# Issuing the second layer's weight loads from SyncE, spread over the first edge slots, in a two-layer graph transformer kernel

## The chip, the cores and the metric

The kernel runs as one program on one core of a Trainium2 chip. The core has five engines that work side by side, each on its own in-order queue of instructions: TensorE (PE, matrix products; its weight loads are listed apart as PEld), VectorE (DVE), ScalarE (ACT), GpSimd (POOL) and SyncE (SP, which issues transfers). Transfers run on 16 DMA engines that all queues share. The metric is the time of one execution on the device in microseconds (us). The kernel before took 2957.67 us, the median of 3 runs (2949.06 to 2958.34).

## The reference

The reference is a graph network with 6250 nodes, 128 features, 100000 edges (sorted by their destination), 16 node types and 32 edge types. Two layers are applied, and then an output product and a normalization:

```
k, q, v = typed_linear(x, ntype, Wk / Wq / Wv)        # one 128x128 matrix per node type
kT = einsum('nhd,htdo->nhto', k, Watt)                # for every node, 8 heads, 32 edge types
vT = einsum('nhd,htdo->nhto', v, Wmsg)
a  = sum(kT[src, :, etype] * q[dst]) * pri[:, etype].T / sqrt(16)
att = softmax of a over the edges of each destination
hag = segment_sum(vT[src, :, etype] * att, dst)
h = silu(typed_linear(hag, ntype, Wa)); h = h * alpha + x * (1 - alpha)
h = layernorm(h) * g + b
# after both layers: out = layernorm(x + (h @ ff_w + ff_b))
```

All data are float32. Each of the two layers has its own Wk, Wq, Wv, Wa, Watt, Wmsg and pri.

## The kernel before

**Tables.** For every node and each of the 32 edge types the kernel stores one row of 256 numbers in HBM: the key already multiplied by Watt and pri, and the value by Wmsg. An edge then needs one row, picked by its source and its type. The table of layer 1 (`tabs[0]`) is made at the start, while the edges are ranked. The table of layer 2 (`tabs[1]`) is made during layer 1: as soon as a block of nodes has its new features, their keys and values and table rows are computed (`nodes`, then `pieces_of` and `table_block`) and stored by GpSimd (line 1915). In the code layer 1 is `l == 0`.

**Weights in SBUF.** There is one set of tiles for both layers. `wkqv[:, 0]` and `wkqv[:, 1]` hold Wk and Wv, `bdk` and `bdv` hold Watt and Wmsg as blocks on a diagonal (the rest is zero, so each is cleared by a memset before it is loaded), and `prit` holds pri. So the second layer's weights can only be loaded when the first layer's table is complete, and they must be there when the first block of layer 1 makes its table rows. `scale_edge_weights` (lines 253 and 254) multiplies `bdk` by `prit` once they are loaded; for the second layer it is written in `nodes`, after the first block's normalization.

**Edges.** Nodes are sorted by type class and by degree into blocks of 128, and a *visit* handles up to four such blocks (a superblock). A *slot* is one edge of each of 128 nodes: GpSimd gathers 128 table rows into one of 50 places of a ring, `kv` (line 1691). VectorE multiplies several slots by the query of the block (line 1707), sums over the 16 numbers of each head (line 1712), takes the softmax with ScalarE's help, multiplies the values by it and adds them up (lines 1518, 1529, 1534). A place of the ring is free again when its values are added. The query of a block is copied to PSUM by ScalarE (line 1471), from a query that TensorE made for the superblock (line 292, copied by ScalarE at lines 1167 and 1171).

**Order.** GpSimd's instructions run in the order in which they are written. The other engines' instructions are put into order by an automatic planner: what is written earlier goes first among what it holds ready, and a later instruction can be pulled up into a gap. Within the visits other work is interleaved with the slots: `spread` enters a generator with a number of steps and a number of slots, and `tick`, called once for each slot, advances the first generator of each list by its share. `work` holds the next queries and the node steps, `pieces` the table rows of layer 2, and `extra` the look-up `looked`. The look-up finds, for the first superblocks of layer 2, which edges come from nodes that will be ready early. It writes two small arrays to HBM (line 1282) and reads them back in many broadcast loads on SyncE (line 1302) that VectorE compares (lines 1326 and 1333). It is spread over 62 slots.

**The loads that the change touches.** After the first table is complete, `tile_gnn_kernel` calls `arm(True)`, which issues Wk and Wv by `load_typed` (line 236) and eight heads' Watt, Wmsg and pri by `load_edge_weights` (lines 245, 246, 248), and then enters `edges()`. These are 2 + 3 x 8 = 26 transfers, for the second layer all on ScalarE's queue. Since they are written ahead of the edges, they are ahead of ScalarE's first copy of a query.

Of the kernel before, what the change touches and what calls it, by code (L numbers as in the profile page):

```python
# [54 lines left out]
HALF = 64  # L55

LOOK = 62.0

OWN_TAILS = {0: ((23, 76, 1, 52),)}

# [33 lines left out]
def kernel(  # L94
# [21 lines left out]
    nc = tc.nc  # L116
# [6 lines left out]
    _, H, RT, HS, _ = Watt.shape  # L123
# [100 lines left out]
    wkqv, wq0, wa = weights[:, :3], weights[:, 3], weights[:, 4]  # L224

    bdk = wts.tile([P, RT, 2 * HS], F32, name="bdk")
    bdv = wts.tile([P, RT, 2 * HS], F32, name="bdv")
    prit = wts.tile([P, RT], F32, name="prit")
# [6 lines left out]
    def load_typed(to, w):  # L235
        nc.scalar.dma_start(to, w.rearrange("t d o -> d t o"))

    def load_edge_weights(l, heads=range(H)):
        if heads[0] == 0:
            nc.vector.memset(bdk, 0.0)  # L240
            nc.vector.memset(bdv, 0.0)
        for h in heads:
            s = slice(h * HS, (h + 1) * HS)
            c = slice((h % 2) * HS, (h % 2 + 1) * HS)
            nc.scalar.dma_start(bdk[s, :, c], Watt[l, h].rearrange("t d o -> d t o"))
            (nc.scalar if l else nc.sync).dma_start(bdv[s, :, c],
                                                    Wmsg[l, h].rearrange("t d o -> d t o"))
            (nc.scalar if l else nc.sync).dma_start(prit[s, :],
                                                    pri[l, h:h + 1, :].to_broadcast([HS, RT]))

    def scale_edge_weights():

        nc.vector.tensor_scalar(prit, prit, 1.0 / float(HS) ** 0.5, None, op0=ALU.mult)
        nc.vector.tensor_tensor(bdk, bdk, prit.unsqueeze(2).to_broadcast([P, RT, 2 * HS]),
                                op=ALU.mult)
# [146 lines left out]
    with tc.manual_schedule(engines={mybir.EngineType.Pool, mybir.EngineType.DVE,  # L402
# [5 lines left out]
        nc.gpsimd.iota(nodef, pattern=[[P, NT]], base=0, channel_multiplier=1,  # L408
                       allow_small_or_imprecise_dtypes=True)
        load_edge_weights(0, range(3))  # L410
        nc.vector.tensor_copy(colf, coli)
        nc.vector.tensor_copy(rowf, rowi)
# [74 lines left out]
        for sl in cuts:  # L487
# [4 lines left out]
            for i in range(sl.start, sl.stop):  # L492
                nc.tensor.matmul(inv_ps, row1[:, i], col1[:, i, :2],
                                 start=(i == 0), stop=(i == NT - 1))
        load_edge_weights(0, range(3, H))
        load_later()
        zeros = pp.tile([P, 2 * D], F32, name="zeros")
# [215 lines left out]
    with tc.manual_schedule(engines={mybir.EngineType.Pool}):  # L713
# [380 lines left out]
        got, stage = [], ""  # L1094
# [22 lines left out]
    def arm(fast):  # L1117
# [56 lines left out]
        def queries0(got, i0, k, types):  # L1174
            ntb, hr = types_of(i0, k), old_rows(xrd, i0, k, "hq")
            yield HOP
            hT = transposed(nps, lambda i: hr[:, i, :], k)
            yield HOP
            ps = nps.tile([P, SB * P], F32, name="nb")
            yield from typed_steps(npl, types, ntb, hT, k * P, [(ps, wq0)])  # L1180
            yield HOP
            q = yield from q_rows(ps, k, "q")
            got.append((q, ntb))
# [44 lines left out]
        def edges():  # L1228
# [160 lines left out]
                nc.vector.tensor_scalar(again, one_bad, 0.0, None, op0=ALU.is_gt)  # L1389
                yield  # L1390

            got, work, pieces, extra = {}, [], [], []
            for _ in queries0(got.setdefault(0, []), *visits[0][1]):
                pass

            def spread(of, gen, steps, slots):

                of.append([gen, steps / slots, 0.0, 1.0])

            def tick(n):  # L1400
                for of in (work, pieces, extra):
                    if of:
                        w = of[0]
                        w[2] += w[1] * n
                        while w[2] >= w[3]:
                            w[2] -= w[3]
                            weight = next(w[0], of)
                            if weight is of:
                                of.pop(0)
                                break  # L1410
                            w[3] = weight or 1.0

            done = []
            spread(extra, looked(), 27, LOOK)

            def rush(of, gen):
                while any(w[0] is gen for w in of):
                    for _ in of.pop(0)[0]:
                        pass
# [185 lines left out]
            for v, (l, (i0, k, types), part, e) in enumerate(visits):  # L1605
# [29 lines left out]
                for i in range(k):  # L1635
# [67 lines left out]
                    for bundle in bundles:  # L1703
                        for (j0, j1, lanes), kv in zip(bundle, [bring(*c[:2]) for c in bundle]):
                            c = j1 - j0
                            kk = kv[:lanes, :, :D]
                            nc.vector.tensor_tensor(  # L1707
                                kk, kk, q[:lanes].unsqueeze(1).to_broadcast([lanes, c, D]),
                                op=ALU.mult)
                            for r in range(c):  # L1710
                                if r == c // 3:
                                    nc.vector.tensor_reduce(  # L1712
                                        a[:lanes, j0:j1, :],
                                        kk.rearrange("p k (h d) -> p k h d", h=H),
                                        axis=AX.X, op=ALU.add)
                                step()
                                tick(1.0)
                            leave(c / CH)
# [311 lines left out]
        if not fast:  # L2030
            for i, w in enumerate((Wk, Wv)):
                load_typed(wkqv[:, i], w[0])
            load_typed(wq0, Wq[0])
            load_typed(wa, Wa[0])
            load_edge_weights(0)
            scale_edge_weights()
            for i0, k in superblocks(NT):
                n = k * P
                hr = old_rows(x, i0, k, "hr")
                nti4 = npl.tile([P, SB * P], I32, name="nti4")  # L2040
                nc.sync.dma_start(
                    nti4[:, :n], ntype[i0 * P:i0 * P + n].unsqueeze(0).to_broadcast([P, n]))
                hT = transposed(nps, lambda i: hr[:, i, :], k)
                outs = [nps.tile([P, SB * P], F32, name="nb") for _ in range(2)]
                typed_linear(npl, range(TY), nti4, hT, n, [(outs[j], wkqv[:, j]) for j in range(2)])
                for j in range(2):
                    to = npl.tile([P, SB * P], F32, name=f"kvT{j}", bufs=2)
                    nc.scalar.copy(to[:, :n], outs[j][:, :n])
                    outs[j] = to
                for i in range(k):  # L2050
                    def store(tg, st, b=i0 + i):
                        nc.sync.dma_start(
                            tabs[0].rearrange("(n g t) c -> g n (t c)", g=TG, t=16)[
                                tg, b * P:(b + 1) * P, :],
                            st.rearrange("p t c -> p (t c)"))
                    for _ in table_block(ep, tps, outs[0], outs[1], i, (), STB, store):
                        pass

        for l in range(L):
            if l == 0:  # L2060
                for i, w in enumerate((Wk, Wv) if fast else (Wk, Wv, Wq)):
                    load_typed(wkqv[:, i], w[1])
                load_edge_weights(1)
                if fast:
                    edges()
                    break
                scale_edge_weights()
            else:
                load_typed(wa, Wa[1])
            edges_any(l)  # L2070

    full = nc.values_load(over[0:1, 0:1], min_val=0, max_val=1)
    with tc.If(full < 1):
        with ExitStack() as ctx2:
            ctx2.enter_context(tc.manual_schedule(engines={mybir.EngineType.Pool}))
            arm(True)
    redo = nc.values_load(again[0:1, 0:1], min_val=0, max_val=1)
    with tc.If(redo > 0):
        with ExitStack() as ctx2:
            arm(False)  # L2080
# [46 lines left out]
```

## Time and profile before

The profile is of one execution, which took 2950.59 us; its span from the first to the last instruction is 2948.7 us.

| what | value |
|---|---|
| median of 3 runs | 2957.67 us (2949.06 to 2958.34) |
| the profiled execution | 2950.59 us, span 2948.7 us |
| GpSimd busy | 1983.6 us, 67% of the span |
| VectorE busy | 1828.0 us, 62% |
| TensorE busy | 1778.6 us, 60%, at a mean granted clock of 0.652 |
| ScalarE busy | 1108.4 us, 38% |
| gathers of layer 1 and 2, line 1691 | 1454 from `ell`, 955 ns each |
| last transfer of the second layer's weights issued by ScalarE | 644.76 us |

Rows of the profile are read as: line of the kernel, engine, operation, output and inputs, shapes, count; then busy time and mean; then the idle time of the engine just before and what ended most of it. In a view by time a row is: start, duration, engine, line, operation, and in brackets the idle time before it. "ACTq" and "SPq" are issues of transfers on ScalarE's and SyncE's queue; they are not counted as busy. "issue" as a releaser is time in which the engine waited for nothing that the profile shows. A wait for several semaphores is put down to the one that came last by the profile; where that one had long been done, it was another.

### The profile page before, as it was taken

To read this page: it belongs to the slowest core of one execution; us is meant where nothing else is said; L and a number is where in the kernel's file an instruction comes from. 1 tells how busy PE (TensorE), PEld (TensorE's weight loads), DVE (VectorE), ACT (ScalarE), POOL (GpSimd) and SP (SyncE) were. 2 spreads that over 40 slices of the span, in tenths; PEclk is the share of its full clock that TensorE was granted. 3 is DMA by queue.
4 is the path that set the end of the run, shared out by engine and by line. 5 is a ranking of instruction groups with operands and counts; after the bars stand their busy time and mean duration, and the time that the engine had idled before them with its cause. 6 is when DMAs were issued, how large, how long until landed. Compare 5 with 4: busy or idle time off the path is not lost. (4 is left out here: it accounts for less than half of the span.)

```text
span 2948.7 us, 22842 instructions
## 1 busy us (share of the span) xinstructions
PE 1778.6 (60%) x5415; PEld 763.8 (26%) x5415; DVE 1828.0 (62%) x4117; ACT 1108.4 (38%) x2580; POOL 1983.6 (67%) x2118
## 2 busy tenths in 40 slices
PE   5999999724676888887587887701433323313121
PEld 2445444411222243232133222200211212101010
DVE  8358323228866777666586655746887767666663
ACT  4876655501423423344243455412332222222220
POOL 5323665566677677777777765767777767777776
PEclk9979766655766656567577566555656656655555
DMA  7998999986667767787787888873333323333331
GB/s 230 403 395 358 385 399 406 396 223 183 217 214 270 272 228 239 266 302 252 257 297 246 287 331 327 306 223 104 105 106 104 107 86 105 106 105 105 106 101 51
DMA packets 186105, 678.28 MB, mean 230 GB/s; under 512 B 55586, under 2 KB 101328, under 8 KB 160912
## 3 DMA queue, kind: packets, MB, share of 16 engines
q0 software_dynamic: 113248, 636.05, 60.8%
q1 hardware_dynamic: 56852, 34.57, 4.3%
q10 hardware_dynamic: 15856, 6.06, 1.0%
q8 instruction: 46, 0.75, 0.1%
q14 instruction: 103, 0.84, 0.1%
HBM read 254.44 MB, written 421.89 MB: 229 GB/s over the span
## 5 line engine op out<-in xcount | busy, mean ns | idle before, releaser
L1691 POOL DMA_INDIRECT kv<-tab,ell x1454 | 1389.2, 955 | 508.5 <-issue 372.6
L323 ACT COPY st<-tb 128x512 f32<-128x512 f32 (+1 forms) x1052 | 717.1, 754 | 540.4 <-PE tb L316 356.2
L1707 DVE TENSOR_TENSOR kv<-kv,tb 128x768 f32<-128x768 f32 (+6 forms) x278 | 262.0, 946 | 534.2 <-DMA kv<-tab,ell 352.8
L292 PE MATMUL nb<-xm,weights 128*128 128x384 f32 (+2 forms) x640 | 368.9, 728 | 351.1 <-DVE xm L275 349.6
L316 PE MATMUL tb<-bdv,kvT 32*128 32x512 f32 x784 | 305.5, 935 | 102.7 <-ACT st L323 99.8
L316 PE MATMUL tb<-bdk,kvT 32*128 32x512 f32 x784 | 294.4, 941 | 35.7 <-ACT st L323 27.7
L316 PE MATMUL tb<-bdv,vT 32*128 32x512 f32 x784 | 290.4, 821 | 33.3 <-ACT st L323 27.5
L292 PEld LDWEIGHTS nb<-xm,weights 128*128 128x128 f32 x640 | 158.8, 269 | 570.9 <-DVE xm L275 359.7
L1712 DVE TENSOR_REDUCE a<-kv 128x48 f32<-128x768 f32 (+6 forms) x278 | 260.0, 939 | 0.7
L1085 POOL DMA_INDIRECT tab<-st,rows x98 | 101.2, 1033 | 199.0 <-ACT st L323 163.0
L1529 DVE TENSOR_TENSOR tb<-kv,tb 128x512 f32<-128x512 f32 (+6 forms) x412 | 228.1, 554 | 2.5
L316 PE MATMUL tb<-bdk,kT 32*128 32x512 f32 x784 | 221.3, 835 | 1.2 <-DVE st L321 0.6
L321 DVE COPY st<-tb 128x512 f32<-128x512 f32 (+1 forms) x124 | 94.1, 759 | 189.7 <-PE tb L316 111.8
L1691 POOL DMA_INDIRECT kv<-tab,ells x166 | 158.9, 957 | 66.9 <-issue 45.9
L1518 DVE TENSOR_TENSOR kv<-kv,tb 128x768 f32<-128x768 f32 (+10 forms) x258 | 192.3, 763 | 0.8
L300 PE MATMUL nb<-ident,hag 128*128 128x128 f32 x98 | 25.9, 406 | 275.5 <-DVE hag L1748 275.5
L275 DVE SCALAR_TENSOR_TENSOR xm<-ntb,nb 128x512 f32<-128x512 bf16 (+2 forms) x224 | 126.7, 593 | 48.1 <-PE nb L300 39.3
L1492 ACT ACTIVATE tb<-a,m 128x17 f32<-128x17 f32 (+12 forms) x328 | 95.3, 290 | 161.9 <-DVE m L1485 153.4
L316 PEld LDWEIGHTS tb<-bdv,vT 32*128 32x128 f32 x784 | 115.0, 230 | 129.8 <-ACT st L323 104.0
L316 PEld LDWEIGHTS tb<-bdv,kvT 32*128 32x128 f32 x784 | 83.5, 255 | 244.4 <-ACT st L323 199.5
L1915 POOL DMA_INDIRECT tab<-st,row x98 | 100.8, 1029 | 67.1 <-ACT st L323 32.7
L316 PEld LDWEIGHTS tb<-bdk,kvT 32*128 32x128 f32 x784 | 80.6, 257 | 181.8 <-ACT st L323 133.9
(395 smaller groups left out, 2274.3 us busy)
## 6 DMA issues: line engine op xcount, KB each, us to landing
kv<-tab,ell POOLq DMA_INDIRECT x1454
weights<-looks SPq DMA_DIRECT2D x40, 128.0 KB
hr<-xrd SPq DMA_DIRECT2D x16, 256.0 KB
kv<-tab,ells POOLq DMA_INDIRECT x166
xrd<-xr POOLq DMA_DIRECT2D x10, 256.0 KB
weights<-looks SPq DMA_DIRECT2D x40, 64.0 KB
hrd<-hs SPq DMA_DIRECT2D x8, 256.0 KB
hr<-xrd SPq DMA_DIRECT2D x10, 192.0 KB
```

Of the source, the lines that this page charges most:

```text
L275: nc.vector.scalar_tensor_tensor(xm[:, :n], ntb[:, :n], float(t), hT[:, :n], op0=ALU.is_equal, op1=ALU.mult)
L292: nc.tensor.matmul(ps[:, :n], w[:, t, :], xm[:, :n], start=(t == types[0]), stop=(t == types[-1]))
L316: nc.tensor.matmul(pt[:, b], yT[s, i * P:(i + 1) * P], bd[s, tt, :], start=True, stop=True)
L323: nc.scalar.copy(to, pt)
L1085: put = nc.gpsimd.indirect_dma_start(out=tabs[0].rearrange("(n t) c -> n (t c)", t=16), out_offset=bass.IndirectOffsetOnAxis(ap=rows1[:, t ...
L1492: nc.scalar.activation(w[:, :, h], av[:, :, h], AF.Exp, scale=-1.0, bias=m[:, h:h + 1], accum_out=den[:, i, h:h + 1])
L1518: nc.vector.tensor_tensor((v_[:, k0:k1] if j or k0 else acc[:, :k1]) .rearrange("p k (h d) -> p k h d", h=H), v_[:, k0:k1].rearrange("p k ...
L1529: nc.vector.tensor_tensor(to, v_, to, op=ALU.add)
L1691: get = nc.gpsimd.indirect_dma_start(out=to.bitcast(I32) if l else to, out_offset=None, in_=tabs[l][:], in_offset=bass.IndirectOffsetOnAxi ...
L1707: nc.vector.tensor_tensor(kk, kk, q[:lanes].unsqueeze(1).to_broadcast([lanes, c, D]), op=ALU.mult)
L1712: nc.vector.tensor_reduce(a[:lanes, j0:j1, :], kk.rearrange("p k (h d) -> p k h d", h=H), axis=AX.X, op=ALU.add)
L1915: put = nc.gpsimd.indirect_dma_start(out=tabs[1].rearrange("(n t) c -> n (t c)", t=16), out_offset=bass.IndirectOffsetOnAxis(ap=row2[:, tg ...
```

## The change

In the fast path the 26 transfers are no longer issued by ScalarE ahead of `edges()`. A new generator `load_next` issues the same transfers from SyncE, one for each step. It is entered in a new list `loads`, which `tick` advances like the others, with 26 steps over 40 slots of layer 1, that is one transfer in about 1.5 slots in the order in which the code is written. The two memsets of `bdk` and `bdv` are written at the start of `edges()`. The other path (`edges_any`, run only for other inputs) loads as before.

```diff
+AT = 40.0
...
+    def load_next():
+
+        for i, w in enumerate((Wk, Wv)):
+            nc.sync.dma_start(wkqv[:, i], w[1].rearrange("t d o -> d t o"))
+            yield
+        for h in range(H):
+            s = slice(h * HS, (h + 1) * HS)
+            c = slice((h % 2) * HS, (h % 2 + 1) * HS)
+            nc.sync.dma_start(bdk[s, :, c], Watt[1, h].rearrange("t d o -> d t o"))
+            yield
+            nc.sync.dma_start(bdv[s, :, c], Wmsg[1, h].rearrange("t d o -> d t o"))
+            yield
+            nc.sync.dma_start(prit[s, :], pri[1, h:h + 1, :].to_broadcast([HS, RT]))
+            yield
...
-            got, work, pieces, extra = {}, [], [], []
+            got, work, pieces, extra, loads = {}, [], [], [], []
+            nc.vector.memset(bdk, 0.0)
+            nc.vector.memset(bdv, 0.0)
             for _ in queries0(got.setdefault(0, []), *visits[0][1]):
                 pass
...
-                for of in (work, pieces, extra):
+                for of in (work, pieces, extra, loads):
...
             spread(extra, looked(), 27, LOOK)
+            spread(loads, load_next(), 2 + 3 * H, AT)
...
             if l == 0:
-                for i, w in enumerate((Wk, Wv) if fast else (Wk, Wv, Wq)):
-                    load_typed(wkqv[:, i], w[1])
-                load_edge_weights(1)
                 if fast:
                     edges()
                     break
+                for i, w in enumerate((Wk, Wv, Wq)):
+                    load_typed(wkqv[:, i], w[1])
+                load_edge_weights(1)
                 scale_edge_weights()
```

## The prediction

> **What bounds the kernel now.** I read the chain of waits first, then the costliest groups, then GpSimd's own instructions in order of time, and last the stretch in which the loads are issued.
>
> ```profile
> span 2948.7 us, 22842 instructions
> POOL 0%; issue 0%
> POOL out_dram L1953 0%
> L1691 POOL DMA_INDIRECT kv<-tab,ell x1454 | 1389.2, 955 | 508.5 <-issue 372.6
> ```
>
> The chain is short and ends on GpSimd (POOL). The group of gathers says why: 1454 gathers of 955 ns, each behind a fixed "issue" gap. In order of time a gather that waits for nothing starts 1.25 us after the one before it. So whatever makes POOL miss that beat is lost, unless a later wait would have swallowed it. The question is where POOL misses it near the moved loads. These are POOL's own rows; the bracket is idle time before the row and what ended it.
>
> ```profile
> 605.21 1.00 POOL L1691 DMA_INDIRECT kv<-tab,ell  x1 [18.77 <-DMA tab<-st,rows]
> ...
> 703.58 0.95 POOL L1691 DMA_INDIRECT kv<-tab,ell  x1 [0.30 <-issue]
> 707.64 0.94 POOL L1691 DMA_INDIRECT kv<-tab,ell  x1 [3.12 <-DVE weights L1326]
> ...
> 719.41 0.94 POOL L1691 DMA_INDIRECT kv<-tab,ell  x1 [4.27 <-DVE tb L1518]
> ...
> 726.41 0.94 POOL L1691 DMA_INDIRECT kv<-tab,ell  x1 [3.56 <-DVE tb L1529]
> ...
> 736.16 2.19 POOL L1691 DMA_INDIRECT kv<-tab,ell  x1 [0.30 <-issue]
> 752.18 1.02 POOL L1915 DMA_INDIRECT tab<-st,row  x1 [13.83 <-ACT st L323]
> ```
>
> From 605.21 to 703.58 the beat holds: (703.58 - 605.21) / 1.25 = 79 gathers. Then 18 gathers, worth 18 x 1.25 = 22.5 us, take until the store at 752.18, that is 48.6 us. **POOL loses 26.1 us there**: the ring of 50 gathered columns is full because VectorE (DVE) has not freed them (3.12, 4.27, 3.56), and then the first store of the second layer's table waits for ScalarE's copy (13.83). After it the beat is nearly held (the last row below: 189 x 1.25 = 236 of 247.8 us), so I take the 26.1 us to carry to the end. Why DVE is late:
>
> ```profile
> 613.66 0.77 ACTq L246 DMA_DIRECT2D bdv<-in_L_gnn_Wmsg_dram  x1
> ...
> 644.76 0.33 ACTq L248 DMA_DIRECT2D prit<-in_L_gnn_pri_dram  x1
> 645.50 0.48 ACT L1167 COPY qT<-nb 128x384 f32<-128x384 f32 x1 [37.62 <-DMA kv<-tab,ell]
> ```
>
> ```profile
> 610.08 3.87 PE L292 MATMUL nb<-xm,weights 128*128 128x384 f32 x8
> ...
> 648.31 0.18 DVE L253 TENSOR_SCALAR prit<-prit 128x32 f32<-128x32 f32 x1 [11.83 <-DMA prit<-in_L_gnn_pri_dram]
> 648.52 1.23 DVE L254 TENSOR_TENSOR bdk<-bdk,prit 128x1024 f32<-128x1024 f32 x1
> 649.67 0.94 DVE L1707 TENSOR_TENSOR kv<-kv,tb 128x768 f32<-128x768 f32 x1
> ```
>
> The query that ScalarE (ACT) is to copy is finished by TensorE at 610.08 + 3.87 = 613.95. ACT copies it at 645.50, since its DMA issues stand ahead. The bracket names a gather, which was long done; the real releaser is ACT's own queue. The first edge product (L1707) follows at 649.67, 44.5 us after the first gather. The busy times by stage, columns us, PE, PEld, DVE, ACT, POOL, then TensorE clock, DMA share and GB/s:
>
> ```profile
> 604.50:649.60 45.10, 8.93 (x29) 5.01 (x29) 10.41 (x35) 2.24 (x9) 33.73 (x36) 0.58 0.91 192
> 649.60:703.60 54.00, 24.53 (x94) 9.39 (x95) 45.53 (x91) 5.23 (x33) 40.90 (x44) 0.56 0.71 204
> 703.60:752.20 48.60, 30.18 (x113) 13.04 (x113) 41.53 (x127) 11.99 (x37) 18.66 (x19) 0.71 0.47 130
> 752.20:1000.00 247.80, 175.61 (x448) 61.77 (x447) 181.47 (x531) 89.07 (x125) 181.57 (x189) 0.66 0.72 247
> ```
>
> DVE works 10.41 of the first 45.1 us and then 87 of 102.6 us, catching up; POOL (18.66) pays at the end of that.
>
> **The change part by part.** *Removed from ACT:* 26 DMA issues (Wk, Wv, and three for each of eight heads). The first is at 584.9, the other 25 end at 644.76 + 0.33 = 645.1. ACT's first copy can then run at 613.95 instead of 645.50: **31.5 us earlier at most**. A lead d of DVE takes min(d, 26.1) from POOL's loss, as the full ring and the late store both count from DVE's first product.
>
> *Wk leaves the stretch before.* POOL's first gather waits 18.77 us for the last stores of the first table, and in that stretch Wk shares the DMA engines with them:
>
> ```profile
> q0 software_dynamic: 514, 6.69, 80.5%
> q10 hardware_dynamic: 528, 1.05, 13.4%
> ```
>
> These are the queues from 584 to 605 us (packets, MB, share of 16 engines): POOL's stores and ACT's Wk, 93.9% together. Without Wk 13.4% of 21 us = 2.8 us of engine time come free, and SyncE (SP) issues nothing there before 604.56. So POOL starts 0 to 2.8 us earlier; 0 if the load goes out early on SP also. I take 2.5, since the engines were nearly full.
>
> *The two memsets* (0.91 us each in this trace, at 604.86 and 605.93) only move in the text; both stay behind the end of the first table. Nothing either way.
>
> *Added to SP:* the same 26 issues, with the DMAs that they start; these are the same bytes through the same 16 DMA engines. SP has other work in the stretch: node types and rows for the first queries, one store of the look-up, and loads of it.
>
> ```profile
> 604.56 0.37 SPq L1153 DMA_DIRECT2D ntb<-typed  x1
> ...
> 611.78 0.25 SPq L1282 DMA_DIRECT2D looks<-lookb  x1
> 622.46 0.33 SPq L1302 DMA_DIRECT2D weights<-looks  x1
> 623.01 0.25 SPq L1282 DMA_DIRECT2D looks<-lookb  x1
> 623.36 9.81 SPq L1302 DMA_DIRECT2D weights<-looks  x11
> ```
>
> What a load costs SP is shown by the first layer's loads on SP at the very start of the kernel, eight of them here and eight of bdv beside them:
>
> ```profile
> L248 SPq DMA_DIRECT2D prit<-in_L_gnn_pri_dram x8: 332/482/487, 9.1 to 22.8; - x8
> L246 SPq DMA_DIRECT2D bdv<-in_L_gnn_Wmsg_dram x8: 311/420/459, 3.3 to 22.4; - x8
> ```
>
> 16 issues in 22.8 - 3.3 = 19.5 us, 1.3 us a piece, where an issue itself is 0.3 to 0.5 us. On ACT the pace from 613.66 to 644.76 (23 issues) was 31.1 / 22 = 1.4 us. So 26 issues hold SP for 34 to 36 us if they go out in one train. Who waits for SP: DVE, for the look-up.
>
> ```profile
> DVE prit L253 <- DMA prit<-in_L_gnn_pri_dram: 11.8, 1, 11.8
> DVE lookb L1280 <- DMA looks<-lookb: 10.7, 1, 10.7
> DVE weights L1326 <- DMA weights<-looks: 10.1, 4, 4.2
> ```
>
> Before 650 us DVE sits 32.6 us on DMA landings. Today that costs nothing: ACT is later still. With ACT's queue gone this cover is gone, and what stands in front of the first product on DVE decides. The text's slots bind that little. Two rows of one look-up step:
>
> ```profile
> 608.16 0.15 DVE L1347 CAST key<-ell 128x25 f32<-128x25 int32 x1
> ...
> 737.45 0.17 DVE L1352 SCALAR_TENSOR_TENSOR key<-flags,key 128x25 f32<-128x25 f32 x1
> ```
>
> L1347 ran 129 us ahead of its neighbour; likewise L253, written after the first block's nodes, ran before the first product. The planner pulls up what it holds ready, so "40 slots" (50 us) may become "at once" on SP; the loads may be ahead of the look-up's store, and L253 may sit among the first products, waiting for the last load. None of this can be read from the trace of before. The bounds of DVE's lead are 31.5 us (nothing waits) and about -20 us (the rival below). I take 16: ACT's release is certain by the rows, about half of it goes to DVE's waits, which stay but no longer all stand ahead of the first product.
>
> The weights' consumers leave room: PE's first product with Wk and Wv is at 738.70, with bdk at 745.72 (rows below), over 90 us after the last issue today.
>
> ```profile
> 738.70 7.09 PE L1866 MATMUL nb<-xm,weights 128*128 128x384 f32 x16 [0.65 <-DVE xm L275]
> 745.72 1.14 PE L316 MATMUL tb<-bdk,kvT 32*128 32x512 f32 x8
> ```
>
> **Sum.** 16 + 2.5 = 18.5 us, of at most 26.1 + 2.8 = 28.9. The profiled execution took 2950.59 us (span 2948.7): 2932.1. The median of the runs shown is 2957.67, 7.1 above it; I forecast a median, so 2957.67 - 18.5 = 2939.2, rounded **2939**.
>
> **The rivals.** *A, the forecast:* lead 10 to 26 us, 2929 to 2945.
>
> *B, the landing holds DVE as the copy did.* The DMA share is 0.91 from 604.5 to 649.6, so the loads land no sooner. 26 issues at 1.3 to 1.4 us from 605 end at 639 to 641; the last row (issued 644.76, seen 648.31) adds 3.6 us, the scaling 1.4: first product at 644 to 646, a lead of 4 to 6, or with two or three products ahead of L253 up to 8. With 0 to 2.5 for Wk, about 6 us: 2952. For it: L253 already stood directly ahead of the first product. Against it: the reason was that ACT had nothing ready before. The Trainium skill ("DMA: Bandwidth & Descriptors", section "Issuing engines are not separate DMA queues") speaks for this case: transfers issued from any engine end on the same 16 DMA engines, and another issuer only saves the sequencer time of issuing. By that rule the gain would be 26 issues of 0.33 us (the prit row), 9 us: 2949, which I count to B, at its end. The trace agrees that the engines were nearly full, but shows ACT held 31 us, over three times the issue times.
>
> *C, slower: the train on SP.* If all 26 issues go ahead of the look-up's store (611.78 today), it goes out at 608 + 35 = 643. From store to the fourth L1326 it is 636.12 - 611.78 = 24 us now (row below), some 12 with emptier queues; then scaling: first product at 657 to 669, a lead of -7 to -19. POOL then loses 7 to 19 us more, 13 in the middle, less 2.5 for Wk: about 2968. It decides from the point where the store goes out later than 649.67 - 14 = 635. For: rows pulled up, as above. Against: the look-up's steps are written between the loads.
>
> ```profile
> 636.12 0.35 DVE L1326 TENSOR_SCALAR weights<-weights,rowk 128x512 bf16<-128x512 bf16 x1 [0.19 <-DMA weights<-looks]
> ```
>
> *D, no use of the lead:* DVE begins early but the store at 752.18 waits as before, because the block's steps are paced by slots. Only the ring's waits go, 3.12 + 4.27 + 3.56 = 11, and come back in the store's wait: 2957. Against: ACT's copy (L323) needs DVE's node steps, which were late as DVE was.
>
> **How the numbers follow.** A 0.52, B 0.28, C 0.12, D 0.08. The time is A's, 2939. The range is 2926 to 2966: low is 28.9 off the median and 3 us for the spread of the runs, high takes B, D and the lower half of C; A's own is 2929 to 2945. This kernel's measurement tells 0.3% (8.9 us) from no change. Faster by more: A, and a fifth of B, 0.57. Within: the rest of B, and D, 0.31. Slower: C, 0.12.
>
> **What would show it.** ACT's L1167 near 614; the first L1707 at about 634 (616 in the best case); POOL's rows around slot 80 to 98 without brackets of 3 to 14 us; the first gather at 602 to 605. B: L253 with a long bracket on prit, between early products. C: the first look-up store after 635 and long brackets on the look-up's landings. The forecast is wrong if POOL's loss goes and the span doesn't fall, or if DVE's first product is not earlier.

## The result and the profile after

| | before | after |
|---|---|---|
| median of 7 runs on the same chip | 2950.02 us (2948.22 to 2958.34) | 2933.86 us (2929.61 to 2942.31) |
| ratio of the runs | | 0.9941, 95% interval 0.9923 to 0.9958 |
| profiled execution, its span | 2950.59 us, 2948.7 us | 2935.60 us, 2933.8 us |
| first gather of layer 1 to first store of its table | 146.97 us | 137.74 us |

The change makes the kernel 16.2 us faster (interval 12 to 23), where 18.5 were forecast. The new time, 2933.86, lies in the forecast's own range. (The forecast, 2939, was taken off 2957.67, the median of the first 3 runs; the 7 runs put the kernel before at 2950.02. Eight of the runs below fell on chips on which the kernel before takes some 3470 us. They are compared with runs on the same chip alone.)

The page of the kernel after ends as the old one did, with GpSimd alone in the chain of waits and the same number of gathers:

```profile
span 2933.8 us, 22834 instructions
...
POOL out_dram L1973 0%
...
L1711 POOL DMA_INDIRECT kv<-tab,ell x1454 | 1386.9, 954 | 494.5 <-issue 378.9
```

(The change adds 20 lines below the new function, so gather L1691 is now L1711, the store L1915 is L1935, the copy of table rows L323 is L340, the first query's copy L1167 is L1184, the product L1707 is L1727.) GpSimd's rows in order of time, of the kernel after; the bracket is idle time and its releaser:

```profile
600.08 1.00 POOL L1711 DMA_INDIRECT kv<-tab,ell  x1 [15.93 <-DMA tab<-st,rows]
...
709.29 0.94 POOL L1711 DMA_INDIRECT kv<-tab,ell  x1 [0.31 <-issue]
...
737.82 1.02 POOL L1935 DMA_INDIRECT tab<-st,row  x1 [16.98 <-ACT st L340]
...
966.50 0.94 POOL L1711 DMA_INDIRECT kv<-tab,ell  x1 [7.88 <-DVE bn L1797]
```

The wait ahead of the first gather fell from 18.77 to 15.93. Between the gather and the store the ring's waits (3.12, 4.27, 3.56) are gone, and the bracket of the store rose from 13.83 to 16.98. The next long wait is 7.88 in both kernels, 229 us behind the store. So what is gained by the store stays: the span ends 2196.5 us behind it before, 2196.0 after.

ScalarE's and VectorE's first rows, and the scaling of pri by the second layer:

```profile
610.38 0.48 ACT L1184 COPY qT<-nb 128x384 f32<-128x384 f32 x1 [26.57 <-DMA kv<-tab,ell]
...
613.37 0.95 DVE L1727 TENSOR_TENSOR kv<-kv,tb 128x768 f32<-128x768 f32 x1 [0.99 <-DMA kv<-tab,ell]
...
720.47 0.37 DVE L270 TENSOR_SCALAR prit<-prit 128x32 f32<-128x32 f32 x1
```

The first product comes 13.3 us behind the first gather, 44.5 before, and it waits for nothing but its own gather; between the two VectorE also waited 5.02 us for TensorE, but for no other load. The scaling, which stood ahead of it, ran 107 us later with no wait. SyncE's queue, in order of time:

```profile
601.02 0.84 SPq L256 DMA_DIRECT2D weights<-in_L_gnn_Wk_dram  x1
...
606.74 3.12 SPq L1299 DMA_DIRECT2D looks<-lookb  x1
609.92 5.01 SPq L261 DMA_DIRECT2D bdk<-in_L_gnn_Watt_dram  x1
...
618.02 2.15 SPq L1319 DMA_DIRECT2D weights<-looks  x4
...
674.76 0.43 SPq L1178 DMA_DIRECT2D hr<-xrd  x1
...
682.80 0.35 SPq L265 DMA_DIRECT2D prit<-in_L_gnn_pri_dram  x1
```

The 26 loads are no train: they stand among the look-up's loads from 601 to 683 us.

**Where the lead went.** VectorE's first product is 31.2 us earlier against the first gather, the store only 9.2. These rows of the kernel before answer for the chain from the first block's normalization (rd) to the store; they come from VectorE's, TensorE's and SyncE's rows in order of time:

```profile
647.01 0.97 SPq L1161 DMA_DIRECT2D hr<-xrd  x2
...
658.13 0.60 PE L300 MATMUL nb<-ident,hr 128*128 128x128 f32 x4
...
709.42 0.30 DVE L1741 RECIPROCAL rd<-den 128x24 f32<-128x24 f32 x1
...
712.52 0.55 DVE L1748 TENSOR_TENSOR hag<-sums,rd 128x384 f32<-128x384 f32 x1
...
713.22 0.90 PE L300 MATMUL nb<-ident,hag 128*128 128x128 f32 x3
```

And the same of the kernel after, from VectorE's, TensorE's, SyncE's and ScalarE's rows:

```profile
672.26 0.30 DVE L1761 RECIPROCAL rd<-den 128x24 f32<-128x24 f32 x1
...
674.90 0.54 DVE L1768 TENSOR_TENSOR hag<-sums,rd 128x384 f32<-128x384 f32 x1
...
680.80 1.11 PE L317 MATMUL nb<-ident,hr 128*128 128x128 f32 x4 [0.49 <-DMA hr<-xrd]
...
691.40 0.66 PE L317 MATMUL nb<-ident,qT 128*128 128x128 f32 x4 [0.34 <-ACT qT L1184]
...
691.93 0.52 PE L317 MATMUL nb<-ident,hag 128*128 128x128 f32 x3
...
715.40 0.46 SPq L1178 DMA_DIRECT2D hr<-xrd  x1
...
719.04 0.98 ACT L1823 ACTIVATE hb<-hr,beta 128x128 f32<-128x128 f32 x3 [3.15 <-DMA hr<-xrd]
...
723.66 8.17 PE L1886 MATMUL nb<-xm,weights 128*128 128x384 f32 x16 [5.62 <-DVE xm L292]
```

rd is 37.2 us earlier. The transposes of hag, the next step, are only 21.3 earlier: they ran 0.7 us behind hag before and run 17.0 us behind it now. Ahead of them on TensorE stands the chain of the next four-block query (hr transposed at 680.80, its last step at 691.40), and that chain's node rows hr left SyncE at 674.76. Before, they had left in the row of 647.01, behind 12 of the look-up's loads; now they leave behind 46 of those and 23 of the moved ones. The matmul with Wk and Wv is 15.0 us earlier (738.70 to 723.66). So of 37.2 us, 16 go between hag and its transposes, 6 on the way to that matmul, and the store keeps 14.4 in absolute time (752.18 to 737.82). Most of the 6 has the same cause. The masked input of that matmul (xm) follows the last transposes (of hs) by 6.0 us now and by 1.0 before. In between ScalarE waits 3.15 us for other node rows, which left SyncE at 715.40, VectorE waits 2.51 us behind ScalarE, and the scaling (1.6 us) now stands there too.

### The profile page after: what moved, and what is told of

Its sections match the earlier page's. It is cut to its first block, busy times and chain, and to the rows that moved or that the text cites. A ratio compares the mean times of both kernels' runs of the same rounds, so it can differ in the third digit from the quotient of the medians.

```text
span 2933.8 us, 22834 instructions
## 1 busy us (share of the span) xinstructions
PE 1786.8 (61%) x5415; PEld 765.8 (26%) x5415; DVE 1830.3 (62%) x4117; ACT 1108.0 (38%) x2578; POOL 1982.0 (68%) x2118
## 5 line engine op out<-in xcount | busy, mean ns | idle before, releaser
L1711 POOL DMA_INDIRECT kv<-tab,ell x1454 | 1386.9, 954 | 494.5 <-issue 378.9
L340 ACT COPY st<-tb 128x512 f32<-128x512 f32 (+1 forms) x1052 | 717.0, 755 | 542.5 <-PE tb L333 342.1
L1727 DVE TENSOR_TENSOR kv<-kv,tb 128x768 f32<-128x768 f32 (+6 forms) x278 | 262.4, 947 | 547.2 <-DMA kv<-tab,ell 374.2
L1711 POOL DMA_INDIRECT kv<-tab,ells x166 | 158.8, 957 | 66.7 <-issue 46.6
L1935 POOL DMA_INDIRECT tab<-st,row x98 | 101.6, 1036 | 70.3 <-ACT st L340 38.4
```

The source lines that it names most:

```text
L340: nc.scalar.copy(to, pt)
L1711: get = nc.gpsimd.indirect_dma_start(out=to.bitcast(I32) if l else to, out_offset=None, in_=tabs[l][:], in_offset=bass.IndirectOffsetOnAxi ...
L1727: nc.vector.tensor_tensor(kk, kk, q[:lanes].unsqueeze(1).to_broadcast([lanes, c, D]), op=ALU.mult)
L1935: put = nc.gpsimd.indirect_dma_start(out=tabs[1].rearrange("(n t) c -> n (t c)", t=16), out_offset=bass.IndirectOffsetOnAxis(ap=row2[:, tg ...
```

## The experiments

Each edit is to the kernel after, unless it says otherwise. "Gather to store" is the time from layer 1's first gather to its first table store, "rd to store" that from the row of rd above to the same store.

**The moved loads issued by ScalarE, in the same slots.**

```
 def load_next():
-    nc.sync.dma_start(...)        # all four
+    nc.scalar.dma_start(...)
```

> The same 26 loads in the same spread places, but issued by ScalarE. Theory (the place in the queue matters, not the engine): ScalarE's first copy is behind two or three issues only, first edge product within 20 us of the first gather, ratio to before 0.990 to 0.996, as the changed kernel (0.994) or a little better, since SyncE is free for the look-up and the node rows. Rival (ScalarE has no room for the issues at all): ScalarE's copies wait behind blocked issues, first product 30 us or more behind the first gather, ratio 0.997 to 1.000.

Measured on a chip where the kernel before takes 3469.2 us: 3467.07, ratio 0.9993 (0.9973 to 1.0012). The rows are the theory's (ScalarE's copy 8.9 us and the first product 20.4 us behind the first gather), the time is the rival's; why the time does not follow the rows on this chip is taken up below, with the changed kernel itself. Again on a second such chip, beside the changed kernel itself:

> The same 26 loads spread over the slots, issued by ScalarE; run again beside the changed kernel. Theory (the place in the queue matters, not the engine): within 0.002 of the changed kernel's ratio on the same chip, plus 0.001 for Wk, which goes out ahead of the last stores again. Rival (ScalarE has no room for the issues): 0.003 or more above the changed kernel.

3470.14 against 3474.0, 0.9985 (0.9959 to 1.001); copy and first product 8.7 and 18.8 us behind the first gather.

**All 26 issued by SyncE in one train, ahead of the first query.**

```
+for _ in load_next():
+    pass
 for _ in queries0(...):
     pass
...
-spread(loads, load_next(), 2 + 3 * H, AT)
```

> All 26 loads on SyncE, written in one train ahead of the edges. Theory (queue order on SyncE matters too; case C of the prediction): the first look-up store goes out 20 to 35 us later than in the changed kernel (606.7), VectorE stands on the look-up's landings behind a few products, the store of the table waits longer than 17 us; ratio 0.997 to 1.005. Rival (leaving ScalarE's queue is all that counts): 0.994 as the changed kernel.

3477.55, ratio 1.0029 (1.0004 to 1.0054).

> All 26 loads on SyncE in one train ahead of the edges; run again beside the changed kernel. Theory (case C of the prediction: a train on SyncE holds the look-up and the scaling holds VectorE): first edge product 30 us or more behind the first gather and ratio 0.004 to 0.010 above the changed kernel. Rival (leaving ScalarE's queue is all that counts): equal to the changed kernel.

3480.81, 1.0007 (0.9979 to 1.0034). SyncE's, VectorE's and ScalarE's rows of the first of the two:

```profile
611.27 0.35 SPq L261 DMA_DIRECT2D bdk<-in_L_gnn_Watt_dram  x1
...
624.11 0.32 SPq L265 DMA_DIRECT2D prit<-in_L_gnn_pri_dram  x1
625.32 0.35 SPq L1170 DMA_DIRECT2D ntb<-typed  x1
```

```profile
629.17 0.18 DVE L270 TENSOR_SCALAR prit<-prit 128x32 f32<-128x32 f32 x1 [14.28 <-DMA ntb<-typed]
```

```profile
637.27 0.48 ACT L1184 COPY qT<-nb 128x384 f32<-128x384 f32 x1 [1.70 <-issue]
```

In a train, the scaling does stand ahead of the first query, as rivals B and C had it: VectorE is idle 14.28 us ahead of it, until loads at and right behind the end of the train land. The first query's copy comes 26.6 us behind the first gather, between the kernel after (10.3) and before (40.3). The first product comes 45.9 us behind it (43.9 in the second run), no earlier than before (44.5), though 14.93 us of that are idle time of a kind that only these chips show ("remote", below). The look-up's first store left at 627.36, as expected, but the wait of the table's store is 13.49, not above 17; and the second run is 0.0008 above the changed kernel on its chip, not 0.004 to 0.010. The 24 loads behind Wk and Wv took SyncE from 611.27 to 624.43, 0.55 us each, not 1.3. (The 1.3 of the kernel's start was a mean over waits: in those 19.5 us SyncE itself waited 5.9, 5.4 and 1.2 us for earlier loads to land, and between these waits its issues stand 0.5 us apart.) Both typed loads are then out ahead of the first gather, whose wait is 22.21.

**Wk alone by ScalarE at its old place, the other 25 as in the change.**

```
-for i, w in enumerate((Wk, Wv)):
-    nc.sync.dma_start(wkqv[:, i], ...)
+nc.sync.dma_start(wkqv[:, 1], Wv[1]...)
...
+    load_typed(wkqv[:, 0], Wk[1])     # ahead of edges()
```

> Wk alone is issued by ScalarE at the old place, the other 25 as in the changed kernel. Theory (Wk takes 2.8 us of the DMA engines from the last stores of the first table): the first gather's wait is 18 to 19 us again instead of 15.9, and the ratio is 0.995, 0.001 above the changed kernel's 0.994. Rival (the shorter wait has another cause): the wait stays at 16 us and the ratio at 0.994.

3487.40, ratio 1.0041 (1.0021 to 1.0062), where 0.995 was expected; on this chip the time again does not decide. Its first gather:

```profile
609.55 1.00 POOL L1710 DMA_INDIRECT kv<-tab,ell  x1 [18.68 <-DMA tab<-st,rows]
```

So the wait goes by what else is loaded in that stretch. It is 18.6 to 18.8 in six profiles with Wk alone there (by ScalarE, at once or in the first slot), 15.7 to 15.9 in six without, and 22.1 to 22.2 in two with Wk and Wv. This term of the forecast, 2.5 us for Wk, is 2.8 to 3.0 between profiles of one chip, on either sort of chip.

**The look-up's broadcast loads issued by ScalarE.**

```
-nc.sync.dma_start(sent[n % ways][rows_, to, :c * P], ...)
+nc.scalar.dma_start(sent[n % ways][rows_, to, :c * P], ...)
```

> The changed kernel, with the look-up's broadcast loads issued by ScalarE. Theory (in the changed kernel the first store's wait of 17 us is there because the node steps stand behind look-up loads that SyncE issues late): the wait falls to 2 to 12 us, ratio 0.989 to 0.992. Rival (the order of VectorE and TensorE sets the node steps, not SyncE's pace): the wait stays at 15 to 19 us, ratio 0.993 to 0.996.

3459.91, ratio 0.9968 (0.9943 to 0.9994).

> The changed kernel with the look-up's broadcast loads issued by ScalarE; run again beside the changed kernel. Theory (the first store's wait of 17 us is there because the node steps stand behind look-up loads that SyncE issues late): wait 2 to 12 us, ratio 0.002 to 0.005 below the changed kernel. Rival (VectorE's and TensorE's order sets the node steps): wait 15 to 19 us, equal to the changed kernel.

3467.93, 0.9981 (0.9957 to 1.0005). The store's wait is 16.05 and 15.90 us, the rival's figure by itself. The changed kernel on the second of these chips, which is next, has 32.60 there, and GpSimd reaches the store at another time; so the two theories are told apart by the chain to the store, in the table below.

**The changed kernel itself, on the second of these chips.**

> The changed kernel itself, beside the kernel before on the same chip, as the reference for the three kernels that run with it. Theory (what was measured at first holds for the program): ratio 0.994 with first edge product 13 us behind the first gather. Rival (on the chip of the first four experiments, where the kernel before took 3469 us and engines stand idle with no releaser named, the change brings nothing): there the ratio is 0.998 to 1.005.

3472.42 against 3474.0, ratio 0.9999 (0.9974 to 1.0023): here the change brings nothing that can be measured. Its page and ScalarE's rows in order of time show a machine that idles in another way:

```profile
span 3488.7 us, 22834 instructions
...
PE 18%; DVE 15%; another core or an unknown queue 15%; issue 14%; POOL 7%; ACT 7%; DMA 2%; DVEq 0%; POOLq 0%; SPq 0%; ACTq 0%
...
L1935 POOL DMA_INDIRECT tab<-st,row x98 | 101.1, 1032 | 367.3 <-ACT st L340 290.4
```

```profile
662.46 0.23 ACT L1336 COPY flags<-tb 128x4 f32<-128x4 f32 x2 [16.51 <-remote]
...
680.10 0.23 ACT L1336 COPY flags<-tb 128x4 f32<-128x4 f32 x2 [17.25 <-remote]
```

The chain no longer ends on GpSimd alone, and GpSimd's stores wait 290.4 us for ScalarE's copies (38.4 in the profile after). There GpSimd's beat is not the bound, so a gain at the first store is not a gain at the end: on the same chip the version with the moved loads on ScalarE has its first store 20.6 us earlier (772.53, below) and takes the same time within the noise. Why the engines idle behind nothing that the profile names is not shown.

The stretch that the lead was lost in can still be compared between these runs, which shared one chip. Rows of the changed kernel there, from VectorE, SyncE, TensorE and GpSimd:

```profile
727.26 0.29 DVE L1761 RECIPROCAL rd<-den 128x24 f32<-128x24 f32 x1
...
729.76 0.43 SPq L1178 DMA_DIRECT2D hr<-xrd  x1
...
729.90 0.54 DVE L1768 TENSOR_TENSOR hag<-sums,rd 128x384 f32<-128x384 f32 x1
...
747.61 0.52 PE L317 MATMUL nb<-ident,hag 128*128 128x128 f32 x3
...
793.14 1.02 POOL L1935 DMA_INDIRECT tab<-st,row  x1 [32.60 <-ACT st L340]
```

The same of the kernel with the moved loads on ScalarE:

```profile
632.74 0.73 SPq L1178 DMA_DIRECT2D hr<-xrd  x1
...
727.24 0.30 DVE L1761 RECIPROCAL rd<-den 128x24 f32<-128x24 f32 x1
...
730.24 0.55 DVE L1768 TENSOR_TENSOR hag<-sums,rd 128x384 f32<-128x384 f32 x1
...
730.96 0.89 PE L317 MATMUL nb<-ident,hag 128*128 128x128 f32 x3
...
772.53 1.02 POOL L1935 DMA_INDIRECT tab<-st,row  x1 [15.81 <-ACT st L340]
```

| profile | moved loads, look-up loads on | hr leaves SyncE, us behind rd | hag to its transposes, us | rd to store, us |
|---|---|---|---|---|
| before | ScalarE ahead, SyncE | -61.8 | 0.7 | 42.8 |
| after | SyncE spread, SyncE | 2.5 | 17.0 | 65.6 |
| after, second chip of 3470 us | SyncE spread, SyncE | 2.5 | 17.7 | 65.9 |
| Wk alone by ScalarE | SyncE spread, SyncE | 6.2 | 14.8 | 66.3 |
| moved loads by ScalarE (both chips) | ScalarE spread, SyncE | -93.8, -94.5 | 0.7, 0.7 | 44.7, 45.3 |
| look-up's loads by ScalarE (both chips) | SyncE spread, ScalarE | -37.1, -38.1 | 0.9, 1.2 | 46.3, 46.0 |
| one train on SyncE (second chip) | SyncE ahead, SyncE | -72.5 | 0.7 | 42.8 |

(hr is the load for the next four-block query; a minus sign means ahead of rd.) Wherever both sets of loads are spread over SyncE's queue (with 62 slots), hr leaves it behind rd, hag's transposes wait 15 to 18 us behind that query's chain, and rd to store takes 66 us. Wherever one of the sets leaves that queue, or goes out ahead of everything, hr is out long before rd and rd to store takes 43 to 46. **So the 20 us that the chain became longer are SyncE's interleaved queue; on the chips of 3470 us this is shown by taking either half away.** On a chip of 2950 us neither half was taken away. There rd comes 72 us behind the first gather, here 110 to 131. With the look-up's loads on ScalarE hr left 89 to 90 us behind the first gather, so that version need not help there; with the moved loads on ScalarE it left 30 to 31 us behind it.

**The kernel before again, for its rows where it takes 3470 us.**

> The kernel before, unchanged, for its own rows beside those of the changed kernel on chips where it takes some 3470 us. There the changed kernel was level with it (0.9999), though its loads moved. Theory 1 (the beat is not what bounds there): before's first product already comes no more than 10 us after that of the changed kernel, because engines stand idle together behind nothing that the profile names, and GpSimd's waits for ScalarE's copy at the later stores of the table sum to some 280 us as they do in the changed kernel; the lead, whatever its size, is used up by those waits before 1000 us. Theory 2 (the change loses elsewhere on these chips): before's first product is 25 to 35 us later than the changed kernel's and the first store some 10 to 15 us later, as in the first comparison, and the changed kernel loses the same amount again at a place that the two traces name. If this run takes 2950 us instead, its rows are those of the profile before and it says nothing new.

It fell on a chip like the first: 2952.75 against 2951.16, ratio 0.9993 (0.9971 to 1.0015). It says nothing of the others, but how well rows repeat: gather to store 146.5 us (146.97 before), rd to store 43.3, the end 2196.8 us behind the store, and the first gather at 608.57 (605.21). So a place in absolute time scatters by 3 us from what lies ahead of it, and the 2.3 us by which the first gather came earlier beyond its wait are not the change's.

**The look-up over 124 slots.**

```
-LOOK = 62.0
+LOOK = 124.0
```

> The changed kernel with the look-up of the second layer's edge lists spread over the first 124 slots instead of 62 (the constant LOOK); nothing is left out. Theory 1 (the remaining wait of some 17 us before the first store of the second layer's table is made by the look-up's work on VectorE, its DMA landings and its place in TensorE's queue, between 640 and 710 us): with half of it per slot that wait falls to below 10 us and the first store comes 8 us or more earlier, and where GpSimd is the bound the time falls by 5 to 9 us against the changed kernel, 0.991 or less against the kernel before. Theory 2 (the wait is made by the order that the planner writes for the first block's nodes, behind the next block's query): the wait stays at 14 to 18 us and the time within 3 us of the changed kernel's. On a chip where the kernel before takes 3470 us the time says little, and the first store's place against the first gather's decides: 135 us or more between them for theory 2, 128 or less for theory 1.

Neither: 2969.04 against 2951.16 on the same chip, ratio 1.0065 (1.0044 to 1.0087). The store's wait grew. Rows from SyncE, ScalarE and GpSimd:

```profile
734.51 22.66 SPq L1319 DMA_DIRECT2D weights<-looks  x35
...
763.77 1.93 ACT L340 COPY st<-tb 128x1024 f32<-128x1024 f32 x2 [1.88 <-PE tb L333]
...
769.38 1.02 POOL L1935 DMA_INDIRECT tab<-st,row  x1 [44.45 <-ACT st L340]
```

The first table's steps are written behind the end of the look-up's pass (`while not done: next(extra[0][0])` in `table`), so what is left of the pass comes in one burst ahead of them. hr, on the other hand, left SyncE behind only 16 of the look-up's loads, 9.1 us ahead of rd, and hag's transposes waited 4.8 us, not 17. The span ends 2196.3 us behind the store again: 31.6 us at the store are 31.9 at the end (2965.7 against 2933.8).

**The look-up over 45 slots.**

```
-LOOK = 62.0
+LOOK = 45.0
```

> The changed kernel with the look-up of the second layer's edge lists spread over the first 45 slots instead of 62; nothing is left out. With 124 slots the first store came 44.5 us late behind ScalarE's copy and the time rose to 2969 us, as the program writes the first table's steps only behind the end of the look-up pass, whose rest then came in one burst (35 broadcast loads in 22.7 us ahead of the first copy). Theory 1 (with 62 slots a rest of the pass, the 20 loads in 13.7 us from 695 us on, still comes as such a burst ahead of the first table, and that is most of the 17 us that GpSimd waits): with 45 slots the burst is gone or half as long, the first store comes 130 to 134 us after the first gather instead of 137.7, and the time is 4 to 8 us below the changed kernel's: 0.991 to 0.993 of the kernel before. Theory 2 (VectorE's work ahead of the first table is the limit, whatever its order): the look-up's steps only move ahead of the early products, the ring of gathered columns is freed later, and the first store stays at 136 to 142 us after the first gather, the time within 4 us of the changed kernel's or above: 0.993 to 0.997.

The store's place is that of theory 2. The first gather and the store:

```profile
597.81 1.00 POOL L1711 DMA_INDIRECT kv<-tab,ell  x1 [15.81 <-DMA tab<-st,rows]
...
735.28 1.02 POOL L1935 DMA_INDIRECT tab<-st,row  x1 [16.36 <-ACT st L340]
```

137.47 us apart, as in the kernel after (137.74), with rd to store 65.5 as well, though the look-up's loads are out by 699 us. A burst at the end of the pass is thus not what the store still waits for with 62 slots. Nor is it in the main VectorE's work, as theory 2 had it, but node rows again. hr left SyncE at 683.60, behind 70 of the look-up's loads, and hag's transposes came 24 us behind hag. Later in the same chain ScalarE waits for the next node rows, and VectorE for ScalarE:

```profile
715.50 0.98 ACT L1823 ACTIVATE hb<-hr,beta 128x128 f32<-128x128 f32 x3 [8.80 <-DMA hr<-xrd]
...
716.94 0.16 DVE L1785 TENSOR_TENSOR t<-rs 128x3 f32<-128x3 f32 x1 [6.60 <-ACT rs L1782]
```

These rows had left SyncE at 711.91, behind a copy within the ring that SyncE had held for 9.9 us until a gather landed. The time was 2943.95 against 2949.81, ratio 0.9979 (0.9962 to 0.9997), outside theory 2's 0.993 to 0.997 and less of a gain than the change as it is; its profiled span, 2933.3, was among the shortest of its runs, so the trace does not show where the typical run loses the rest.

**The same with the kernel before.**

```
-LOOK = 62.0
+LOOK = 45.0          # in the kernel before
```

> The kernel before (the 26 loads by ScalarE ahead of its first copy) with the look-up spread over 45 slots instead of 62; nothing is left out. Theory 1 (the end of the look-up pass in slots is what the first store waits for, in both kernels): the first store comes 3 to 8 us earlier than the 147 us after the first gather that the kernel before shows, and the time is 0.997 to 0.999. Theory 2 (in the kernel before VectorE is late from its first product on, so that an earlier look-up only takes the place of products): the ring's waits of some 12 us grow and the store's wait shrinks by as much, the first store stays at 145 to 149 us, and the time is the same, 0.999 to 1.002.

2961.23 against 2949.81, ratio 1.0037 (1.002 to 1.0054): worse than either theory. GpSimd's rows:

```profile
696.03 0.95 POOL L1691 DMA_INDIRECT kv<-tab,ell  x1 [6.86 <-DVE weights L1326]
...
760.44 1.02 POOL L1915 DMA_INDIRECT tab<-st,row  x1 [14.18 <-ACT st L323]
...
997.73 0.94 POOL L1691 DMA_INDIRECT kv<-tab,ell  x1 [14.23 <-DVE bn L1777]
```

Where VectorE starts late, an earlier look-up does take the place of products: the ring's waits are longer, gather to store is 151.5 us instead of 146.5 to 147.0, the store's own wait does not shrink, and a later wait grows from 7.88 to 14.23. The changed kernel took the same edit with no loss at the store. That is the lead, seen from the other side.

## Why the prediction was right, point by point

- **What bounds the kernel: right.** In five of the six traces in which GpSimd is the bound, the end stood 2196 to 2198 us behind the first store. The sixth, the kernel before with 45 slots (2205), has the extra waits behind the store that its rows show. What is gained or lost at the store arrives at the end.
- **ACT's release: right.** Its copy was to come near 614 and came at 610.38.
- **VectorE's lead: mis-sized.** 16 us were taken, between -20 and 31.5; it was 31.2, the upper bound. Of the waits for loads that VectorE had ahead of the first product, only that for the gather was left: the scaling, which had stood ahead of it, was not pulled up this time.
- **What the lead is worth to GpSimd: the step that failed.** The prediction let a lead d take min(d, 26.1), ring and store alike. By that rule 31.2 would have given 26.1 (27.0, if the 96 gathers that the trace has up to the store are counted); it gave 9.2. The ring's 10.95 us went whole. The store's wait did not go: it rose from 13.83 to 16.98, because the moved loads, spread among the look-up's on SyncE, put the next query's hr behind them. The prediction named node rows among SyncE's work, but counted only the look-up's loads as waited for. So twice the lead that was taken, and a third of it kept: 9.2 where 16 stood in the sum. Two errors in opposite directions stand in this term, and that the forecast came as near as it did is in part luck.
- **Wk: right**, 2.84 us in the trace against 2.5, and shown, for GpSimd's wait, by the run that puts it back.
- **The sum.** 9.23 + 2.84 = 12.1 us are the change's by the rows; the profiled executions differ by 15.0, of which 2.3 came from ahead of the stretch. The medians' difference, 16.2, has an interval of 12.4 to 22.7, which the 12.1 falls just short of; what the rest is, scatter or a gain elsewhere, these runs don't tell.
- **Rival B: refuted** (L270 at 720.47, without a wait). With it falls, for this case, the estimate that went by the Trainium skill, "DMA: Bandwidth & Descriptors", section "Issuing engines are not separate DMA queues": the loads share the DMA engines as it says (Wk beside GpSimd's stores, 2.8 us), but moving them brought ScalarE's copy 30 us forward against the first gather (40.3 to 10.3), not the 9 us of 26 issue times. The 9 was low, too: the 26 issues on ScalarE last 14.7 us in the trace (one alone 4.06), and the rest of the 30 is time in which an issue, and all behind it, stood in ScalarE's queue. By the trace's semaphores, 17 of the last 25 went out right behind the landing of an earlier load, 9 of these one of the look-up's transfers, which SyncE had issued. The place in the order counts more than the issuer: in the same slots on ScalarE the copy came 8.7 and 8.9 us behind the first gather, in the train on SyncE 25.4 and 26.6.
- **Rival C: refuted** for the change (store of the look-up at 606.74, not 643), and its price was too high: the train took 0.55 us an issue, since the 1.3 to 1.4 were means over waits. Where GpSimd isn't the bound it was 0.3% and 0.1% slower than the kernel before, the second not clear of none. What it costs where GpSimd is the bound was not run.
- **Rival D: half right.** The ring's waits went and the store's stayed, as it said, but of 11 us only 3.15 came back. Its reason, the pace by slots, holds for the look-up's end (124 slots), not for what remained with 62.

**Open.** Why the same program takes 2934 us on one chip and 3472 on another; and what a version brings that keeps hr out of that queue where GpSimd is the bound. An estimate from rows: rd at 672.26 and the 45.3 us of the runs with the loads on ScalarE would have the store ready at 717.6, ahead of its turn at 737.82 - 16.98 = 720.84, so up to 17 us more. On the chips of 3470 us that version was no faster than the change.

## What to carry to other kernels

When loads move to another queue, list everything else that queue carries in the stretch, and who stands behind each: here the look-up on SyncE was watched and the node rows of the next query, on the same queue, made the chain to the store 20 us longer. A lead of a feeding engine is worth only what the next fixed wait leaves of it, so cost the wait that ends last (the store) on its own chain, apart from the one that goes first (the ring). Where one place carries to the end (2196 us behind the first store), measure differences between two events of one trace, which repeat within half a microsecond here, and not absolute times, which scatter by three.

## What the runs showed of the hardware

- The kernel before takes 2950 us on some chips (three comparisons) and 3470 on others (two). In the slower sort, up to 600 us the engines do the same work (GpSimd 286.1 us busy on both); from then on they idle together for 10 to 17 us at a time, with releasers that the profile calls remote or issue, and GpSimd is busy 97 instead of 139 us from 600 to 800 us (the windows of the changed kernel on either). This change, which helps GpSimd's beat, is worth 0.6% on the one sort and nothing measurable on the other.
- A load of 1.05 MB (Wk) beside GpSimd's last stores of the first table lengthens the wait for them by 2.8 to 3.0 us, Wv with it by another 3.5 (15.8, 18.7, 22.2).
- SyncE's issues of the same kind of load stand about 0.5 us apart both at the start of the kernel and in the train at 611 us (0.55). The mean of 1.3 us at the start contains 12.5 us in which SyncE waited for earlier loads to land: a mean pace over a stretch is not what an issue takes.
